# Key rows of both directions by seven block products, all but one ahead of the first burst of key matmuls

## The chip, the cores and the metric

The kernel runs on one core of a Trainium2 chip. The metric is the device time of one execution in microseconds. Three runs of the kernel before took 551.29, 551.41 and 551.92 us, a median of 551.41. Engines are named as in the profile: PE is TensorE's matmuls and PEld its weight loads, DVE is VectorE, ACT is ScalarE, POOL is GpSimd, and SP is the engine that issues most DMAs.

## The reference, cut to what matters

The inputs are `x` (16 batches of 512 nodes with 512 features), a condition vector for each batch, and a mask of 16 x 512 x 512 x 11 labels. For each of two directions, graph attention goes to the first 20 nodes only:

```
row_zero  = x.sum(-1) == 0
self_feat = concat(x, where(row_zero, 0, q)) @ W_self.T + b_self
output = self_feat
for d in range(2):
    A  = adj or adj transposed, first 20 columns      # 16 x 512 x 20 x 11
    vb = A @ w_bias + b_bias
    kv = self_feat[:, :20]
    qh = (self_feat @ Wq[d].T + bq[d])   in 16 heads of 32
    kh = (kv        @ Wk[d].T + bk[d])   in 16 heads of 32
    aff = where(A.sum(-1) > 0, qh . kh / sqrt(32), -9e15) + vb
    w   = softmax(aff over the 20)
    output += (w @ kv) @ Wout[d] per head + bout[d]
result = x + relu(output)
```

All of it is in float32. The change is about `kh`, the key rows, which are computed once for all batches.

## The kernel before, in words

**The whole.** A setup builds everything that the batches share, and then a loop runs over 16 batches. The order of the instructions on every engine is written out by hand (`manual_schedule`): an engine takes its instructions in the order in which the program emits them, and waits only for its operands and for the buffer that it writes.

**The setup.** Features lie on the 128 partitions in four chunks. The self features of the 16 x 20 = 320 key nodes come first: `kv_terms` (L767) multiplies `xkv` by the self weights `ws_v`; POOL and DVE multiply a flag by the projected condition (`qp`, L801); DVE adds the two (`kvn`, L805) and subtracts from each batch's nodes its first node (`kvD`, L809), which leaves 16 x 19 = 304 columns in four chunks. `kvT` (ACT, L813) is a copy with the bias for the value path.

**The key rows.** `key_rows(d, jc)` (L818) makes 128 rows of the keys of direction `d`: 4 chunks of 128 input features, each by four matmuls of 32 output columns, on 304 columns (L825); DVE then takes them out of PSUM into `khD` (L831). There are eight such blocks, two directions of four. Four of them are made ahead of the first burst, with the first three chunks of all four first; the other four go between the bursts 1 to 4.

**The bursts.** The keys must be multiplied by the query weights `wq_sb`, head by head. That is cut into 20 bursts (`keys`, L908). A burst fills four PSUM banks in two pairs (tags `s0` and `s1`, one buffer each), and then ACT takes one pair out (L939) and DVE the other (L941) into a staging tile `st`, which SP stores in DRAM (L946, L948) and whose part for batch 0 POOL copies (L945). The pairs have one buffer each, so the next burst starts when both are out. Between two bursts TensorE does something else from a plan written as letters: `m` bias terms (`bias_terms`, L838, DVE alone: query weights times the self bias, summed; they need `wq_sb` and `br_sb`), `b` their end (`biases`, L844, L846), `c` bias scores (L856), `v` and `w` pieces of the value products (`values`, L883), `n` row flags (L222), and `p` the seven block products of batch 0's self features (L284). When a value block is complete DVE takes it out (`value_pieces`, L896) and POOL's queue stores it (L900).

**Seven block products** are what the kernel uses already for the self features and for the scores: the matrix is cut in 2 x 2 blocks of 256 features by half the columns, and seven products of block sums replace eight. For that, `weight_sums` (L227 to L234) makes four sums of the self weight blocks on POOL, `ws_s`, between the `qp` multiplies and the row sums of batch 0 (`row_sums`, L215, L217). The `khD` rows of the changed kernel are made in the same way.

**What sets the order around the change.** On POOL: `rsk` (L761, L763), `qp` (L801), the four weight sums, `row_sums(0)`, then copies and stores between the bursts. On DVE: `qp`, `kvn` and `kvD` in turn, `qwD` (L814), the four `khD` rows, then the evictions of the bursts with bias terms and `khD` rows between them. On SP: the loads in the order in which they stand at L737 to L758, then `bo_rows` (L997) and the stores of the bursts.

Of the kernel before, what the change touches and what calls it, by code (L numbers as in the profile page):

```python
# [18 lines left out]
def gat_kernel(  # L19
# [99 lines left out]
    def load_adj(b, h, ins=None, ts=slice(0, 2)):  # L119
        if ts.start == 0:  # L120
            adjs[b, h] = load.tile([P, 2, S * L], I32, tag="adj", name=f"adj{b}_{h}", bufs=3)
        a = adj[b, h * 2 * P : (h + 1) * 2 * P].rearrange("(t p) d m l -> p t (d m l)", p=P)
        behind(nc.sync.dma_start(adjs[b, h][:, ts], a[:, ts]), ins)
# [100 lines left out]
        nc.vector.tensor_scalar(nzs[b], ps[:, :N], 0.0, None, ALU.not_equal)  # L224


    def weight_sums():  # L227

        (a11, a12), (a21, a22) = [[ws_v[:, 2 * j : 2 * j + 2, bass.ts(i, F // 2)] for j in range(2)] for i in range(2)]
        s1, s2, s3, s4 = (ws_s[:, i] for i in range(4))  # L230
        nc.gpsimd.tensor_add(s1, a21, a22)
        nc.gpsimd.tensor_sub(s2, s1, a11)
        nc.gpsimd.tensor_sub(s3, a11, a21)
        nc.gpsimd.tensor_sub(s4, a12, s2)  # L234

    def half(l):
        return slice(NG + l * HN, NG + (l + 1) * HN)
# [451 lines left out]
    with tc.tile_pool(name="setup", bufs=1) as sp, tc.tile_pool(name="ps_acc", bufs=4, space=PSUM) as acc["pool"]:  # L689
# [16 lines left out]
        kvD = sfp.tile([P, C, N], F32, tag="sf", name="kvD")[:, :, : B * ND]  # L706

        with tc.tile_pool(name="setup_k", bufs=1) as sk:
            xkv = sk.tile([P, C, BM], F32, name="xkv")
# [49 lines left out]


            nc.gpsimd.tensor_add(rsk, xkv[:, 0], xkv[:, 1])  # L761
            for k in range(2, C):
                nc.gpsimd.tensor_add(rsk, rsk, xkv[:, k])  # L763
            kv_ps = [bank(f"ps_kv{fc}") for fc in range(C)]

            def kv_terms(fc, k):
# [28 lines left out]
            )  # L795
            for fc in range(C):
                kv_terms(fc, 3)
            for fc in range(C):
                qp = sk.tile([P, B, NG], F32, tag="qp", name=f"qp{fc}", bufs=4)
                engine = nc.gpsimd if fc else nc.vector  # L800
                engine.tensor_mul(  # L801
                    qp, nzk.rearrange("p (b m) -> p b m", m=NG),
                    qw[:, fc].unsqueeze(2).to_broadcast([P, B, NG]),
                )
# [4 lines left out]
                nc.vector.tensor_sub(  # L809
                    kvD[:, fc].rearrange("p (b m) -> p b m", m=ND), each[:, :, 1:],  # L810
                    each[:, :, :1].to_broadcast([P, B, ND]),
                )
                nc.scalar.activation(kvT[:, fc], kvn[:, fc], AF.Identity, bias=bs_sb[:, fc : fc + 1])  # L813
            nc.vector.tensor_sub(qwD, qw[:, :2], qw[:, 2:])  # L814
            weight_sums()
            row_sums(0)

            def key_rows(d, jc, ks=range(C)):  # L818

                if ks[0] == 0:  # L820
                    of[d, jc] = bank(f"ps_k{d}{jc}")
                ps = of[d, jc]
                for k in ks:
                    for a in range(HL):
                        nc.tensor.matmul(  # L825
                            ps[bass.ts(a, R), : B * ND], wk_sb[d][:, k, bass.ds(jc * P + a * R, R)], kvD[:, k],
                            start=(k == 0), stop=(k == C - 1),
                        )
                if ks[-1] == C - 1:
                    by = bk_sb[:, d, jc : jc + 1]  # L830
                    nc.vector.tensor_scalar(khD[:, d * C + jc], ps[:, : B * ND], by, by, ALU.add, ALU.subtract)  # L831

            of = {}

            def bias_terms(d, c):

# [5 lines left out]
            def biases():  # L842

                nc.vector.tensor_add(bqw, bqw, bq_sb)  # L844
                for hl in range(HL):
                    nc.scalar.activation(  # L846
                        bqbd[bass.ts(hl, DH), :, :, hl], bqw[bass.ts(hl, DH)], AF.Copy, scale=SCALE
                    )

        with tc.tile_pool(name="setup_g", bufs=3) as sg:  # L850

# [98 lines left out]
            def block_product(n):  # L950
# [8 lines left out]


            steps = {
                "b": [(biases, ())],
                "c": [(bias_scores, (d,)) for d in range(2)],
                "m": [(bias_terms, (d, c)) for c in range(C) for d in range(2)],
                "n": [(row_flags, (b,)) for b in range(2)],
                "p": [(block_product, (n,)) for n in (1, 2, 6, 7, 5, 4, 3)],
                "v": [(values, (t, (d,), k)) for t in range(2) for d in range(2) for k in range(C)],
                "w": [(values, (2, (0, 1), k)) for k in range(C)],
            }
# [13 lines left out]
            rest = [(d, hg) for hg in range(C) for d in range(2)]  # L983
            first = None
            for r, k in ((0, 0), (1, 0), (0, 1), (1, 1), (2, 0), (2, 1), (0, 2), (1, 2), (3, 0), (3, 1), (2, 2), (3, 2)):
                key_rows(*rest[r], (k,))
            for r in range(4):
                key_rows(*rest.pop(0), (C - 1,))
            for n, runs in enumerate(bursts):
                for i in range(len(rest)):  # L990
                    if (i < 1 and n > 0) or any(fc == 0 and (d, hg) == rest[0] for fc, hg, d, _, _ in runs):
                        key_rows(*rest.pop(0))
                if n in (3, 4):
                    values(*steps["v"].pop(0)[1])
                if n == 0:
                    bo_rows = load.tile([P, C, N], F32, tag="x2", name="bo_rows", bufs=1)
                    nc.sync.dma_start(bo_rows[:, :2], bout.partition_broadcast(P))  # L997
# [6 lines left out]
                if rest:  # L1004
                    for kind in "mm" if n else ():
                        f, args = steps[kind].pop(0)
                        f(*args)
                    continue
                first = n if first is None else first
                for kind in plan[n - first] if n - first < len(plan) else ():  # L1010
                    f, args = steps[kind].pop(0)
                    f(*args)
                if n == first:
                    for d in range(2):
                        nc.gpsimd.tensor_add(br_sb, br_sb, bo_rows[:, d])
                if n > first:
                    value_pieces()
                if n == 7:
                    mask_mul(0, 0)
                if n == 8:  # L1020
# [376 lines left out]
```

## Time and profile before

| | |
|---|---|
| median of three runs | 551.41 us (551.29 to 551.92) |
| the profiled execution | 552.17 us |
| its span, first to last instruction | 550.3 us |
| mean granted TensorE clock | 0.996 |
| PE busy | 540.9 us (98%) |
| DVE busy | 480.0 us (87%) |
| POOL busy | 436.4 us (79%) |
| ACT busy | 404.4 us (73%) |
| first key row matmul | at 17.41 us |
| first burst | at 25.81 us |
| last product of the setup ends | at 92.11 us |

The span is counted from the first to the last instruction on the core; the execution's own time has some 1.9 us around it. Times of rows are microseconds from the span's start. A float32 matmul has two records in the trace, so 128 records are 64 matmuls. Weight loads (PEld) go on beside matmuls. The chain of waits is followed back from the last instruction, each step to what released it.

### The profile page before, as it was taken

How to read it: one execution, taken by the hardware profiler on the slowest of the kernel's cores; microseconds unless marked ns; L12 is line 12 of the kernel's file. 1: busy time of each engine (PE TensorE's matmuls, PEld its weight loads, DVE VectorE, ACT ScalarE, POOL GpSimd, SP SyncE). 2: the span in 40 equal slices, each digit the busy share in tenths (PEclk: the TensorE clock that was granted, in tenths of full speed). 3: DMA queues.
4: the chain of work that ended last, by engine and by line, in shares of the span. 5: the costliest groups of instructions: out<-in, count | busy, mean ns of one | idle time of the engine just before them, and what ended most of it. 6: DMA issues, size and time to landing. Idle time of an engine off the chain costs nothing.

```text
span 550.3 us, 19621 instructions
## 1 busy us (share of the span) xinstructions
PE 540.9 (98%) x7908; PEld 424.1 (77%) x7908; DVE 480.0 (87%) x708; ACT 404.4 (73%) x1000; POOL 436.4 (79%) x421
## 2 busy tenths in 40 slices
PE   9999999999999999999999999999999999999994
PEld 6554367888787878788888888887878788888783
DVE  0775678888989999999999999999999999999995
ACT  1125345798797988888888888887878787877663
POOL 2636896779979797979888888888897979797665
PEclk9999999999999999999999999999999999999998
DMA  8999999978887877878776767686777587736034
GB/s 301 375 396 350 306 357 348 298 224 242 227 253 210 219 229 224 231 209 234 208 237 181 241 188 222 203 228 192 231 207 212 175 252 189 229 103 187 2 117 154
DMA packets 100530, 126.45 MB, mean 230 GB/s; under 512 B 19592, under 2 KB 68678, under 8 KB 98392
## 3 DMA queue, kind: packets, MB, share of 16 engines
q1 hardware_dynamic: 98696, 121.93, 71.4%
q0 software_dynamic: 1168, 2.23, 1.7%
q8 instruction: 62, 1.02, 0.8%
q10 hardware_dynamic: 576, 1.05, 0.5%
q14 instruction: 28, 0.23, 0.1%
HBM read 86.23 MB, written 40.24 MB: 230 GB/s over the span
## 4 chain that ended last, share of the span: by engine, by line
PE 92%; DVE 4%; POOL 2%; issue 1%; ACT 0%; DVEq 0%; POOLq 0%; ACTq 0%
PE ps_f L657 30%; PE ps_a L397 23%; PE ps_c L397 11%; PE ps_d L397 6%; PE ps_o_f L567 5%; PE ps_v L883 3%; PE ps_k L825 3%; PE ps_o_c L567 2%; PE ps_kv L767 1%; PE ps_a L284 1%; PE ps_l L397 1%; POOL w L536 1%; PE ps_c L284 1%; PE ps_warm L727 1%; DVE cond L332 1%
## 5 line engine op out<-in xcount | busy, mean ns | idle before, releaser
L327 ACT ACTIVATE prod<-adj,wb_sb 128x80 f32<-128x80 int32 x330 | 116.0, 429 | 0.0
L536 POOL TENSOR_TENSOR w<-w,sm 128x640 f32<-128x640 f32 x63 | 80.3, 1274 | 30.6 <-DVE sm L532 29.4
L657 PE MATMUL ps_f<-t,ws_s 128*64 128x246 f32 x720 | 80.0, 371 | 0.0
L657 PEld LDWEIGHTS ps_f<-t,ws_s 128*64 128x64 f32 x720 | 51.8, 137 | 18.9
L527 ACT ACTIVATE w<-w 128x640 f32<-128x640 f32 x60 | 43.8, 730 | 18.5 <-DVE w L523 18.5
L544 DVE STREAM_TRANSPOSE wt<-w 128x640 f32<-128x640 f32 x63 | 52.5, 833 | 1.5 <-POOL w L536 1.4
L657 PE MATMUL ps_f<-x,ws_v 128*64 128x246 f32 x480 | 52.4, 371 | 0.0
L531 DVE TENSOR_REDUCE sm<-w 128x32 f32<-128x640 f32 x63 | 51.0, 810 | 1.1 <-ACT w L527 1.0
L522 DVE TENSOR_REDUCE ps_d<-w 128x32 f32<-128x640 f32 x59 | 48.7, 826 | 1.8 <-ACT ps_d L431 0.2
L523 DVE TENSOR_TENSOR w<-w,ps_d 128x640 f32<-128x640 f32 x59 | 48.4, 821 | 2.0
L657 PEld LDWEIGHTS ps_f<-x,ws_v 128*64 128x64 f32 x480 | 34.7, 137 | 13.0
L370 POOL TENSOR_TENSOR k<-g,k 128x608 f32<-128x608 f32 x30 | 44.7, 1490 | 0.0
L397 PEld LDWEIGHTS ps_a<-g,sf 128*64 128x64 f32 x544 | 34.2, 137 | 5.9 <-issue 5.8
L397 PE MATMUL ps_a<-g,sf 128*64 128x152 f32 x544 | 38.6, 295 | 0.0
L567 PE MATMUL ps_o_f<-wt,vd 32*32 32x256 f32 (+3 forms) x708 | 37.8, 383 | 0.3 <-ACT ps_o_f L554 0.3
L338 DVE TENSOR_REDUCE add<-prod 128x80 f32<-128x960 f32 x32 | 36.7, 1148 | 1.5 <-POOL prod L333 1.5
L397 PE MATMUL ps_d<-g,sf 128*64 128x152 f32 x544 | 37.9, 293 | 0.0
L346 ACT COPY both<-add 64x80 f32<-64x80 f32 x128 | 32.6, 255 | 5.7 <-DVE add L338 4.6
L567 PE MATMUL ps_o_c<-wt,vd 32*32 32x256 f32 (+1 forms) x720 | 36.8, 386 | 0.0
L672 POOL TENSOR_TENSOR t<-x,t 128x492 f32<-128x492 f32 x30 | 34.8, 1161 | 1.2
L333 POOL TENSOR_SCALAR prod<-cond 128x80 f32<-128x80 f32 x32 | 18.0, 564 | 22.1 <-DVE cond L332 20.8
L397 PEld LDWEIGHTS ps_d<-g,sf 128*64 128x64 f32 x544 | 35.3, 137 | 0.2 <-ACT sf L675 0.2
(298 smaller groups left out, 1437.8 us busy)
## 6 DMA issues: line engine op xcount, KB each, us to landing
g<-g_d SPq DMA_DIRECT2D x60, 304.0 KB
g_d<-st SPq DMA_DIRECT2D x16, 1064.0 KB
out_T<-o SPq DMA_DIRECT2D x63, 256.0 KB
x<-in_xT SPq DMA_DIRECT2D x56, 256.0 KB
xn<-in_xn SPq DMA_DIRECT2D x48, 256.0 KB
adj<-in_adj SPq DMA_DIRECT2D x52, 220.0 KB
vd<-bd_d SPq DMA_DIRECT2D x64, 64.0 KB
nz<-nz_d SPq DMA_DIRECT2D x14, 256.0 KB
```

What stands on the lines that cost most here:

```text
L327: nc.scalar.activation(p[:, :, l], a[:, :, l], AF.Identity, scale=wb_sb[:, l : l + 1])
L338: done["masks"] = nc.vector.tensor_reduce(add, prods.pop((b, h)), AX.X, ALU.add)
L370: done["ksum"] = engine.tensor_sub(to, one, two)
L397: nc.tensor.matmul(slot(g)[bass.ts(p, P // 2), : HL * S].rearrange("p (h m) -> p h m", m=NG)[:, :, 1:], of(k)[:, bass.ds(first + g * P // ...
L522: nc.vector.tensor_reduce(mx, f, AX.X, ALU.max)
L523: done["weigh"] = (engine or nc.vector).tensor_sub(f, f, mx.unsqueeze(2).to_broadcast([P, per, NG]))
L527: done["exp"] = nc.scalar.activation(t, t, AF.Exp)
L531: nc.vector.tensor_reduce(sm, heads(weighs[b, c, l]), AX.X, ALU.add)
L536: done["normal"] = nc.gpsimd.tensor_mul(f, f, smalls.pop((b, c, l)).unsqueeze(2).to_broadcast([P, per, NG]))
L544: done["turn"] = nc.vector.transpose(wts[b][:, c, l], weighs.pop((b, c, l)).rearrange("p g w -> p (g w)"))
L567: nc.tensor.matmul(outsum[b][a][bass.ds(at // 2 * DH, n * DH), bass.ds(c * N // 2 + lo * P, (hi - lo) * P)].rearrange("p (n r) -> p n r", ...
L657: nc.tensor.matmul(parts[b][n in (2, 3, 5)][bass.ts(a, P // 2), bass.ts(i, HN)], lhs, x[:, k], start=False, stop=k == 1, skip_group_check= ...
```

## The change

The key rows are made by seven products for each direction, cut like the self features: two halves of the input features, two halves of the output features, two halves of the 304 columns (152 each). `key_product(d, n)` is 8 matmuls of 128 x 64 weights on 152 columns; `key_rows(d, n)` adds product `n` into `khD` in two pieces, on ACT for products 1, 6 and 7, on DVE for 2, 5, 3 and 4. The products 1, 6, 7 and 4 share one PSUM bank, 5 and 3 another, 2 has one of its own. Four differences of `kvD` blocks (`kv_sum`, DVE) and four sums of weight blocks for each direction (`weight_sum`, POOL) are new.

Thirteen of the fourteen products stand ahead of the first burst, with all eight bias terms between them on DVE; the fourteenth follows burst 0. The sums of the self weights move behind bursts 3 to 6, in the buffer that held direction 0's key sums. The loads are in another order, and batch 1's `x` is loaded after the key products, because direction 1's key sums use its buffer. The value pieces start with burst 0 in place of burst 3.

```
-    def weight_sums():
-        (a11, a12), (a21, a22) = ...
-        nc.gpsimd.tensor_add(s1, a21, a22)
-        nc.gpsimd.tensor_sub(s2, s1, a11)
-        nc.gpsimd.tensor_sub(s3, a11, a21)
-        nc.gpsimd.tensor_sub(s4, a12, s2)
+    def weight_sum(w, s, n):
+        (a11, a12), (a21, a22) = [[w[:, 2 * j : 2 * j + 2, bass.ts(i, F // 2)] for j in range(2)] for i in range(2)]
+        if n == 1:
+            nc.gpsimd.tensor_add(s[:, 0], a21, a22)
+        else:
+            nc.gpsimd.tensor_sub(s[:, n - 1], *{2: (s[:, 0], a11), 3: (a11, a21), 4: (a12, s[:, 1])}[n])
...
+        wk_s = [ws_s, load.tile([P, 4, 2, F // 2], F32, tag="x1", name="wk_s1", bufs=1)]
...
             nc.sync.dma_start(br_sb, b_row.partition_broadcast(P))
+            nc.sync.dma_start(bq_sb, bq)
             load_x(0)
-            nc.sync.dma_start(wb_sb, w_bias.partition_broadcast(P))
-            load_adj(0, 0)
-            nc.sync.dma_start(bq_sb, bq)
-            nc.sync.dma_start(bb_sb, b_bias.partition_broadcast(P))
             for d in range(2):
                 rows(wo_sb[:, d], woT[d])
-            load_x(1)
+            bo_rows = load.tile([P, C, N], F32, tag="x2", name="bo_rows", bufs=1)
+            nc.sync.dma_start(bo_rows[:, :2], bout.partition_broadcast(P))
+            nc.sync.dma_start(wb_sb, w_bias.partition_broadcast(P))
+            nc.sync.dma_start(bb_sb, b_bias.partition_broadcast(P))
+            load_adj(0, 0)
             load_adj(0, 1)
             nc.gpsimd.tensor_add(rsk, xkv[:, 0], xkv[:, 1])
             for k in range(2, C):
                 nc.gpsimd.tensor_add(rsk, rsk, xkv[:, k])
+            for n in (1, 2):
+                weight_sum(wk_sb[0], wk_s[0], n)
...
+            def kv_sum(n):
+                one, two = {
+                    1: lambda: (kv_block(0, 1), kv_block(0, 0)), 2: lambda: (kv_block(1, 1), kv_sums[1]),
+                    3: lambda: (kv_block(1, 1), kv_block(0, 1)), 4: lambda: (kv_block(1, 0), kv_sums[2]),
+                }[n]()
+                nc.vector.tensor_sub(kv_sums[n], one, two)
             for fc in range(C):
...
+                if fc == 2:
+                    kv_sum(1)
+            for n in (2, 3, 4):
+                kv_sum(n)
+            for d, n in ((1, 1), (1, 2), (0, 3), (1, 3), (0, 4), (1, 4)):
+                weight_sum(wk_sb[d], wk_s[d], n)
-            nc.vector.tensor_sub(qwD, qw[:, :2], qw[:, 2:])
-            weight_sums()
             row_sums(0)
...
+            def key_product(d, n, ks=range(2)):
+                w, x = {
+                    1: ((0, 0), kv_block(0, 0)), 2: ((0, 1), kv_block(1, 0)), 3: (3, kv_block(1, 1)),
+                    4: ((1, 1), kv_sums[4]), 5: (0, kv_sums[1]), 6: (1, kv_sums[2]), 7: (2, kv_sums[3]),
+                }[n]
+                to = key_ps[d, "d" if n == 2 else "c" if n in (3, 5) else "a"]
+                for k in ks:
+                    for i in range(2):
+                        for a in range(2):
...
+                            nc.tensor.matmul(to[bass.ts(a, P // 2), bass.ts(i, KN)], lhs, x[:, k], ...)
+            def key_rows(d, n):
+                for i in range(2):
...
+                    if n == 4:
+                        nc.vector.tensor_scalar(to, ps, by, by, ALU.add, ALU.subtract)
+                    elif n in (1, 6, 7):
+                        nc.scalar.activation(to, ps, AF.Identity, bias=by)
+                    else:
+                        nc.vector.scalar_tensor_tensor(to, to, by, ps, ALU.subtract, ALU.add)
...
+            for k in range(2):
+                for d in range(2):
+                    key_product(d, 1, (k,))
+                    if k:
+                        key_rows(d, 1)
+            for n in (2, 6, 7, 5, 3):
+                for d in range(2):
+                    key_part(d, n)
+                    for _ in range({6: 2, 7: 1, 5: 1}.get(n, 0)):
+                        bias_terms(*terms_left.pop(0))
+            nc.vector.tensor_sub(qwD, qw[:, :2], qw[:, 2:])
+            for d in range(2):
+                nc.gpsimd.tensor_add(br_sb, br_sb, bo_rows[:, d])
+            key_part(0, 4)
+            biases()
...
-            plan = "mmvv bvv vvc vvc vvn vvw vw vw wn p p p p p p p".split()
+            plan = "kv vv vv vc vc vv vv vv vv vw ww wn n p p p p p p p".split()
...
             for n, runs in enumerate(bursts):
...
                 if n == 0:
-                    bo_rows = ...; nc.sync.dma_start(bo_rows[:, :2], bout.partition_broadcast(P))
+                    load_x(1)
                 keys(runs)
...
+                if 2 < n < 7:
+                    weight_sum(ws_v, ws_s, n - 2)
```

More of the change, by code (lines that the diff above doesn't have):

```diff
@@ L797, in gat_kernel, with kv_block @@
                 kv_terms(fc, 3)
+            KN = B * ND // 2
+            def kv_block(j, l):
+                return kvD[:, 2 * j : 2 * j + 2, bass.ts(l, KN)]
+            kv_sums = {n: sk.tile([P, 2, KN], F32, name=f"kv_t{n}") for n in range(1, 4)}
+            kv_sums[4] = kv_all[:, :2, B * ND : B * ND + KN]
+            def kv_sum(n):
[4 more added lines that the diff above has]
+                nc.vector.tensor_sub(kv_sums[n], one, two)
             for fc in range(C):
@@ L833, in gat_kernel @@
-            of = {}
+                if fc == 2:
[4 more added lines that the diff above has]
+                weight_sum(wk_sb[d], wk_s[d], n)
+            row_sums(0)
+            key_ps = {(d, "a"): bank(f"ps_k{d}") for d in range(2)}
+            for i, key in enumerate("dc"):
+                t = ps_s.tile([P, 2, 512], F32, tag=f"s{i}", name=f"ps_k{key}", bufs=1)
+                key_ps.update({(d, key): t[:, d] for d in range(2)})
@@ L848, in biases @@
                     )
+            terms_left = [(d, c) for c in range(C) for d in range(2)]
+            for k in range(2):
[13 more added lines that the diff above has]
+            biases()
         with tc.tile_pool(name="setup_g", bufs=3) as sg:
@@ L961, in gat_kernel @@
             steps = {
[L962 removed]
+                "k": [(key_part, (1, 4))],
                 "c": [(bias_scores, (d,)) for d in range(2)],
[L964 removed]
                 "n": [(row_flags, (b,)) for b in range(2)],
@@ L1003, in gat_kernel @@
                 value_pieces()
[L1004 to L1010, printed above, removed]
+                for kind in plan[n]:
                     f, args = steps[kind].pop(0)
                     f(*args)
[L1013 to L1017, printed above, removed]
+                value_pieces()
+                if 2 < n < 7:
+                    weight_sum(ws_v, ws_s, n - 2)
                 if n == 7:
```

47 lines of the change are left out of this document (19 added, 28 removed).

## The prediction, made before the result was known

> **What bounds the kernel now.** I read the busy shares of the page first, then the busy time by stretch of the start, then the chain of waits through it, then the DVE and POOL timelines of the stretch that the change rebuilds.
>
> ```profile
> span 550.3 us, 19621 instructions
> PE 540.9 (98%) x7908; PEld 424.1 (77%) x7908; DVE 480.0 (87%) x708; ACT 404.4 (73%) x1000; POOL 436.4 (79%) x421
> ```
> ```profile
> 20.00:25.00 5.00, 5.00 (x84) 2.60 (x80) 3.05 (x5) 0.56 (x1) 3.61 (x3) 1.00 1.05 381
> 25.00:30.00 5.00, 5.00 (x88) 2.72 (x76) 3.32 (x6) 1.07 (x2) 3.24 (x3) 1.00 1.07 373
> 30.00:35.00 5.00, 5.00 (x84) 2.58 (x83) 4.66 (x11) 2.21 (x5) 2.05 (x4) 1.00 1.05 384
> 75.00:80.00 5.00, 5.00 (x64) 3.54 (x64) 3.69 (x6) 3.04 (x6) 4.99 (x8) 1.00 1.02 347
> ```
> After the length of a stretch come PE, PEld, DVE, ACT and POOL busy. PE fills the start while DVE has 2 us of every 5 free until 30 us. So TensorE time saved is span saved, as long as TensorE isn't made to wait.
>
> ```profile
> 17.41 8.39 PE ps_k L825 x128
> 25.81 0.46 PE s_g(0, 0, 0, 0, 16)0_325 L917 x2
> ...
> 37.61 2.18 PE ps_k L825 x32
> ...
> 41.67 1.85 PE ps_v L883 x16
> ...
> 49.68 0.51 PE ps_c L856 x8
> ...
> 69.85 0.86 PE ps_nz L222 x8
> ...
> 92.11 2.22 PE ps_a L397 x32
> 94.33 2.07 PE ps_d L397 x32
> ```
> Start, length, what. The key rows start at 17.41, the first burst at 25.81, the last setup product ends at 92.11. Half the key rows (8.39) lie ahead of the first burst, the other four blocks (2.18 each, 8.72) between bursts.
>
> **The change, part by part.**
>
> *TensorE work.* Old: 8.39 + 8.72 = 17.1 us. New: 14 parts (seven products, two directions) of 8 matmuls, 128x64 against 152 columns. The score product at L397 has this very form: 2.07 us for 32 records, two a matmul, so 1.035 for eight. 14 x 1.035 = 14.5: 2.6 us less. 13 parts (13.5 us) go ahead of the first burst, so without a wait it starts at 17.41 + 13.5 = 30.9.
>
> *What they wait for.* This decides. Four block differences of kvD are new on DVE, with both inputs in SBUF, and the eight bias terms (L838, also two SBUF inputs) now stand ahead of the first burst. POOL gets two sums of the first key weights ahead of its qp multiplies, and six more behind them. So two-input DVE work meets a full POOL queue. What happens then the trace shows:
>
> ```profile
> 15.27 0.49 DVE L801 TENSOR_TENSOR qp<-nzk,qw 128x320 f32<-128x320 f32 x1
> 16.39 0.97 DVE L809 TENSOR_TENSOR kvD<-kvn 128x304 f32<-128x304 f32 x1
> 17.80 0.48 DVE L809 TENSOR_TENSOR kvD<-kvn 128x304 f32<-128x304 f32 x1
> 18.71 1.04 DVE L809 TENSOR_TENSOR kvD<-kvn 128x304 f32<-128x304 f32 x1
> 20.19 1.04 DVE L809 TENSOR_TENSOR kvD<-kvn 128x304 f32<-128x304 f32 x1
> 21.16 1.26 DVE L814 TENSOR_TENSOR qwD<-qw 128x32 f32<-128x32 f32 x1
> ```
> ```profile
> 11.16 0.86 POOL L763 TENSOR_TENSOR rsk<-rsk,xkv 128x320 f32<-128x320 f32 x1 [3.48 <-DMA xkv<-in_xkvT]
> 15.31 2.64 POOL L801 TENSOR_TENSOR qp<-nzk,qw 128x320 f32<-128x320 f32 x3 [3.29 <-DVE qw L792]
> 17.91 1.51 POOL L231 TENSOR_TENSOR ws_s<-ws_v 128x512 f32<-128x512 f32 x1
> 19.50 1.40 POOL L232 TENSOR_TENSOR ws_s<-ws_s,ws_v 128x512 f32<-128x512 f32 x1
> 20.86 1.51 POOL L233 TENSOR_TENSOR ws_s<-ws_v 128x512 f32<-128x512 f32 x1
> 22.34 1.28 POOL L234 TENSOR_TENSOR ws_s<-ws_v,ws_s 128x512 f32<-128x512 f32 x1
> 26.60 1.28 POOL L215 TENSOR_TENSOR rx<-x 128x512 f32<-128x512 f32 x1 [2.99 <-DMA x<-in_xT]
> ```
> The same kvD subtract takes 0.48 or 1.04. Each long one ends 0.33 behind the end of a POOL sum: 18.71 + 1.04 = 19.75, L231 ends 19.42; 20.19 + 1.04 = 21.23, L232 ends 20.90. The tiny L814 takes 1.26 and ends 0.05 behind L233 (22.37). So a two-input DVE instruction sits out the POOL instruction under way, runs 0.33, and POOL's next runs 1.15 behind it (19.75 to 20.90, 21.23 to 22.37). The bias term does so too:
>
> ```profile
> 43.10 0.64 POOL L945 COPY g<-st 128x152 f32<-128x152 f32 x1 [4.02 <-DVE st L941]
> ```
> ```profile
> 34.66 0.68 DVE L838 SCALAR_TENSOR_TENSOR bqt<-wq_sb,br_sb 128x512 f32<-128x512 f32 x1
> 35.27 0.68 DVE L838 SCALAR_TENSOR_TENSOR bqt<-wq_sb,br_sb 128x512 f32<-128x512 f32 x1
> 43.50 0.79 DVE L838 SCALAR_TENSOR_TENSOR bqt<-wq_sb,br_sb 128x512 f32<-128x512 f32 x1
> ```
> POOL ends at 43.74, this term at 44.29, 0.55 later; alone they follow each other in 0.61.
>
> *When POOL can start.* From the key inputs' last quarter (11.16) to x0 (26.60) 5.77 MB land (0.26 self weights, 2.1 key and 2.1 query weights, 0.26 bias, 1.05 x0, by the tiles' sizes), 374 GB/s. The first key weights, 1.31 MB behind 11.16, land at 14.7. The qp multiplies, at 15.31 now, wait for the two sums. With 1.25 for the first sum, 1.2 (between the 1.15 and 1.28 above) for the others, 0.77 a multiply ((2.64 - 0.33)/3), and one DVE instruction let in after each:
>
> | POOL (ends) | DVE let in behind it (ends) |
> |---|---|
> | key sums 1, 2 of direction 0 (16.0, 17.5) | qp0 (16.3), kvD0 (17.8) |
> | qp1, qp2, qp3 (18.6, 19.4, 20.5) | kvD1 (19.7), kvD2 (20.8) |
> | six key sums (22.0, 23.5, 25.05, 26.6, 28.1, 29.65) | difference 1 (22.3), kvD3 (23.85), differences 2, 3, 4 (25.4, 26.9, 28.45) |
>
> kvD3 is done at 23.85 in place of 21.23, and TensorE waits for it. The bound is then DVE's own row of work behind difference 4, whose short pieces cost by these rows:
>
> ```profile
> L297 DVE SCALAR_TENSOR_TENSOR sf<-nz,qw,ps_a 128x246 f32<-128x246 f32 x8 | 3.4, 467 | 1.6 <-PE ps_a L284 1.0 <-PE ps_a L289 0.6
> ```
> One PSUM input, no waiting for POOL: 0.467 at 246 columns, less 94 columns at 0.33/304 us each, gives 0.37 at 152, a pair about 0.6 (an estimate: two overlap a little). Then: two pairs of product 2 (28.45 to 29.7); bias terms 1 to 3, each let in behind one of the three row sums of x0 (L215: 30.85 POOL, 31.4; 33.1; 34.85); terms 4 to 6 alone (3 x 0.61: 36.7); product 5's pair, a term, its other pair, a term, product 3's two pairs (6 x 0.6: 40.3). Product 3 shares product 5's bank, so TensorE stops at 31.6 until 37.3; its two parts and the first direction's product 4 end at 40.65. That is the first burst's start: 9.75 behind 30.9.
>
> *The other edits.* ACT takes products 1, 6 and 7 out of PSUM in two pieces; TensorE has the other direction's 1.035 meanwhile: nothing (without that cover, some 0.8 a part, two pieces at about the 0.4 of DVE's above). Moving the first self-weight sums to bursts 3 to 6 puts 5.1 us (4 x 1.28) on POOL beside them and takes the bout adds out; POOL is full at 75 to 80 (4.99 of 5), so if that cover is short its x sums are late: 0 to 2.5, taken 0, because TensorE waits for POOL nowhere in these rows. The loads are put in another order on SP; x1 now waits there for the last key sum's reader, with only the g stores of later bursts behind it: nothing. Bursts: the evictions of one must end before the next, and these rows price it:
>
> ```profile
> 37.71 1.28 DVE L941 TENSOR_SCALAR st<-_g(0, 2, 0, 14, 16)1_450 128x76 f32<-128x76 f32 x3 [1.24 <-PE _g(0, 2, 0, 14, 16)1_450 L917]
> ```
> That burst ended at 37.61, so 1.4 us of other TensorE work are wanted between two. Two value pieces give 1.85 (L883), one and a bias score 0.93 + 0.51 = 1.44; burst 12 has only the row flags, 0.86 (the L222 row): 0.5 lost.
>
> *Sum.* First burst 40.65 - 25.81 = 14.84 later; 8.72 fewer between the bursts; the last part there 1.04; burst 12 0.5: **+7.65 us**. Profiled execution 552.17 (span 550.3, 1.9 around it), 0.76 over the median of 551.41. 552.17 + 7.65 - 0.76 = **559.1** as a median.
>
> *What the Trainium skill says.* SBUF — State Buffer, "Who interferes with whom": a VectorE instruction with two SBUF inputs contends with a GpSimd one that reads SBUF, and issue order decides who is shut out entirely. By that rule a waiting DVE instruction goes next, as in my table: +7.65. The trace mostly agrees, but once it doesn't:
>
> ```profile
> 92.79 1.49 POOL L370 TENSOR_TENSOR k<-g,k 128x608 f32<-128x608 f32 x1
> 94.23 1.07 POOL L672 TENSOR_TENSOR t<-x 128x492 f32<-128x492 f32 x1
> ```
> ```profile
> 92.86 3.00 DVE L377 TENSOR_TENSOR f<-sf 128x512 f32<-128x512 f32 x1
> ```
> DVE waited through two POOL instructions (95.30 + 0.56 = 95.86). Two such losses would add 2.3 to the sum, which I keep for the range.
>
> **The rivals.**
>
> *A half-lifted cover.* DVE gets in twice per POOL instruction as often as once. For: 0.48 at 17.80, which waited only 0.15. Against: L814. Without any waiting kvD3 comes at 21.23 as now, and TensorE has half a part and ten more behind it, 10.5 x 1.035: first burst at 32.1. Half way to my 40.65 is 36.4: 10.59 - 8.72 + 1.04 + 0.5 = **+3.4, 554.8**.
>
> *No waiting at all.* First burst at 32.1: 6.29 - 8.72 + 1.04 + 0.5 = **-0.9, 550.5**, no change that can be told. For it: DVE is idle 2 us of 5 now, so its work alone has room. Against it stand the long subtracts above.
>
> *TensorE never waits* and burst 12 costs nothing: 30.9, so 5.09 - 8.72 + 1.04 = **-2.6, 548.8**, faster. It decides only if POOL and DVE both finish ahead of TensorE; POOL's eleven instructions from 14.7 on speak against it.
>
> *The clock falls in the gap.* TensorE idles from 31.6 to 37.3 in my working. At the end of the kernel:
>
> ```profile
> 545.00:546.00 1.00, 0.00 (x0) 0.00 (x0) 1.00 (x4) 0.08 (x1) 0.72 (x1) 1.00 0.71 270
> 546.00:547.00 1.00, 0.00 (x0) 0.00 (x0) 0.54 (x2) 0.00 (x0) 0.00 (x0) 0.53 0.59 221
> ```
> the granted clock is 0.53 in the second microsecond without a matmul. Three parts at half speed cost 3 x 1.035 = 3.1 more: **+10.75, 562.2**. Against: the idle is broken up if DVE is quicker. The Trainium skill, TensorE: Matmul & The Clock Gate, Part 1, names an idle window of about 3.4 us for the drop to half rate; a gap of 5.7 would be over it, which is this rival.
>
> **How the numbers follow.** Forecast 0.55; clock 0.17; half-lifted 0.13; no waiting 0.08; never waits 0.07. A measurement can tell about 0.2%, 1.1 us, from no change. Slower 0.55 + 0.17 + 0.13 = 0.85, the same 0.08, faster 0.07. The range reaches from below the half-lifted case to just over the clock's, 553.3 to 562.6, which leaves out the 0.15 of the two quick cases and a little; the forecast's own is 557 to 561.4 (the two lost turns at its top).
>
> **What would show it.** Kv differences and late kvD subtracts on DVE of 1 us and more, each ending 0.33 behind a POOL sum; TensorE idle before product 2's second half and before product 3, put down to DVE; the first burst near 40; between bursts fewer gaps but one of half a microsecond at the second row flags. It is wrong if the differences take 0.48 each, or if the first burst comes before 34.

## The result, and the profile after

The changed kernel took 565.50 us (median of 4 runs, 564.35 to 565.93), the kernel before beside it 551.66 us (4 runs, 551.29 to 552.12): a ratio of 1.0247, with a 95% interval of 1.0235 to 1.026. The change makes the kernel 13.8 us slower. The sign was forecast; the size was not: 559.1 was predicted, and the range ended at 562.6.

The profiled execution took 565.08 us; the page gives its span and busy time.

```profile
span 563.2 us, 19606 instructions
PE 542.1 (96%) x7876; PEld 431.6 (77%) x7876; DVE 486.6 (86%) x720; ACT 408.4 (73%) x1012; POOL 446.9 (79%) x429
```

The span is 12.9 us longer (563.2 against 550.3), and PE's share fell from 98% to 96%. The busy time by stretch shows where; after the stretch's length come PE, PEld, DVE, ACT and POOL busy, the granted clock, the DMA share and GB/s.

```profile
20.00:25.00 5.00, 1.58 (x22) 1.02 (x18) 4.93 (x5) 1.68 (x6) 4.92 (x4) 1.00 1.06 380
25.00:30.00 5.00, 2.13 (x18) 2.00 (x20) 2.82 (x4) 0.00 (x0) 4.92 (x5) 0.59 1.05 388
30.00:35.00 5.00, 5.00 (x59) 4.74 (x57) 4.71 (x13) 1.67 (x6) 2.59 (x2) 0.72 0.87 307
75.00:80.00 5.00, 3.53 (x48) 1.85 (x44) 3.75 (x6) 1.42 (x5) 3.82 (x5) 1.00 1.01 366
...
25.00:26.00 1.00, 0.00 (x0) 0.00 (x0) 1.00 (x2) 0.00 (x0) 1.00 (x2) 0.97 1.04 389
26.00:27.00 1.00, 0.00 (x0) 0.00 (x0) 1.00 (x1) 0.00 (x0) 1.00 (x2) 0.50 1.06 395
...
32.00:33.00 1.00, 1.00 (x12) 0.95 (x10) 1.00 (x1) 0.67 (x2) 0.67 (x1) 0.61 1.04 357
```

PE was full in all four stretches before (5.00 of 5). Now it works 3.7 of the 10 us from 20 to 30, while DVE and POOL are full until past 27; and its clock is halved from 25.94 (0.97 of that microsecond is 0.94 at full speed and the rest at half) to 32.78 (0.61, counted the same way). From 75 to 80 it lacks 1.5 us again. PE's waits, in total, their number and the longest:

```profile
PE ps_kd L863 <- DVE khD L880: 4.2, 1, 4.2
PE ps_kc L863 <- DVE khD L880: 2.6, 3, 0.9
PE ps_kd L863 <- DVE kvD L829: 2.1, 1, 2.1
...
PE _g(2, 0, 1, 10, 16)1_782 L985 <- DVE st L1009: 1.5, 1, 1.5
...
PE _g(2, 2, 0, 14, 16)0_854 L985 <- ACT st L1007: 0.2, 1, 0.2
```

L863 are the key products; `ps_kd` holds product 2 of both directions, `ps_kc` products 5 and 3 of both. PE's timeline (start, length, what, and in brackets the idle time before and who ended it):

```profile
22.94 0.74 PE L863 MATMUL ps_kd<-kvD,wk 128*64 128x152 f32 x8 [2.10 <-DVE kvD L829]
27.87 2.29 PE L863 MATMUL ps_kd<-kvD,wk 128*64 128x152 f32 x16 [4.20 <-DVE khD L880]
29.95 2.24 PE L863 MATMUL ps_k<-kv_t,ws_s 128*64 128x152 f32 x16
...
35.49 1.23 PE L863 MATMUL ps_kc<-kv_t,ws_s 128*64 128x152 f32 x16
37.55 1.25 PE L863 MATMUL ps_kc<-kv_t,wk_s 128*64 128x152 f32 x16 [0.83 <-DVE khD L880]
...
44.03 0.53 PE L985 MATMUL s_g(0, 0, 0, 0, 16)0_422<-khD,wq_sb 32*128 32x304 f32 x2
...
45.08 1.25 PE L863 MATMUL ps_k<-kvD,wk 128*64 128x152 f32 x16
46.27 1.07 PE L951 MATMUL ps_v<-wo_sb,kvT 128*32 128x512 f32 x8
...
104.95 2.29 PE L396 MATMUL ps_a<-g,sf 128*64 128x152 f32 x32
```

And DVE and POOL, which TensorE waits for:

```profile
21.86 1.02 DVE L829 TENSOR_TENSOR kvD<-kvn 128x304 f32<-128x304 f32 x1
22.92 1.43 DVE L816 TENSOR_TENSOR kv_t<-kvD,kv_t 128x304 f32<-128x304 f32 x1
24.27 1.53 DVE L816 TENSOR_TENSOR kv_t<-kvD 128x304 f32<-128x304 f32 x1
25.72 1.53 DVE L816 TENSOR_TENSOR kvD<-kvD,kv_t 128x304 f32<-128x304 f32 x1
27.17 0.64 DVE L880 SCALAR_TENSOR_TENSOR khD<-khD,bk_sb,ps_kd 128x152 f32<-128x152 f32 x2
30.29 0.66 DVE L880 SCALAR_TENSOR_TENSOR khD<-khD,bk_sb,ps_kd 128x152 f32<-128x152 f32 x2 [2.47 <-PE ps_kd L863]
...
31.47 1.75 DVE L889 SCALAR_TENSOR_TENSOR bqt<-wq_sb,br_sb 128x512 f32<-128x512 f32 x1
...
75.94 0.69 DVE L964 SCALAR_TENSOR_TENSOR v<-br_sb,ps_v 128x512 f32<-128x512 f32 x1 [3.33 <-DMA vw_d<-v]
```
```profile
21.18 1.38 POOL L233 TENSOR_TENSOR wk_s<-wk_s,wk 128x512 f32<-128x512 f32 x1
22.51 1.50 POOL L233 TENSOR_TENSOR ws_s<-wk 128x512 f32<-128x512 f32 x1
23.97 1.49 POOL L233 TENSOR_TENSOR wk_s<-wk 128x512 f32<-128x512 f32 x1
...
26.88 1.50 POOL L233 TENSOR_TENSOR wk_s<-wk,wk_s 128x512 f32<-128x512 f32 x1
...
66.26 1.50 POOL L968 DMA_DIRECT2D vw_d<-v  x2
```

Direction 0's product 2 is done at 23.68. Direction 1's does not begin before 27.87, right behind the row pieces at 27.17 with which DVE took direction 0's out. Those stood on DVE behind the four block differences. After that the roles change: DVE's next piece (30.29, 2.47 us idle before it) waits for direction 1's product. Direction 1's product 2 needs neither `khD` rows nor any result of DVE that was late. What it shares with them is the tile.

So the first burst starts at 44.03 where it was 25.74 before and 40.65 was predicted. From there to the first score product of the loop (L396) 60.92 us pass; they were 66.31 before (L397, 92.05), and the prediction had 59.1. These are starts in the timeline, which all runs are compared by. The rows that the prediction shows (25.81 and 92.11) are of a view that puts the same starts 0.06 or 0.07 later; in that view the changed kernel has 44.10 and 105.02.

### The profile page after: what moved, and what is told of

It reads as the page before. It is cut to its first block, busy times and chain, and to the rows that moved or that the text cites. A ratio compares the mean times of both kernels' runs of the same rounds, so it can differ in the third digit from the quotient of the medians.

```text
span 563.2 us, 19606 instructions
## 1 busy us (share of the span) xinstructions
PE 542.1 (96%) x7876; PEld 431.6 (77%) x7876; DVE 486.6 (86%) x720; ACT 408.4 (73%) x1012; POOL 446.9 (79%) x429
## 3 DMA queue, kind: packets, MB, share of 16 engines
q8 instruction: 62, 1.02, 0.8%
## 4 chain that ended last, share of the span: by engine, by line
PE 84%; DVE 5%; POOL 4%; DMA 4%; issue 2%; ACT 1%; SPq 0%; DVEq 0%; POOLq 0%; ACTq 0%
PE ps_f L656 29%; PE ps_a L396 22%; PE ps_c L396 10%; PE ps_d L396 6%; PE ps_o_f L566 5%; DMA wk<-in_wkT 2%; PE ps_k L863 2%; DMA vw_d<-v 2%; PE ps_o_c L566 1%; PE ps_v L951 1%; PE ps_a L283 1%; PE ps_kc L863 1%; PE ps_l L396 1%; POOL cq_d L935 1%; POOL w L535 1%
## 5 line engine op out<-in xcount | busy, mean ns | idle before, releaser
L396 PEld LDWEIGHTS ps_a<-g,sf 128*64 128x64 f32 x544 | 34.2, 137 | 5.9 <-issue 5.8
L396 PE MATMUL ps_a<-g,sf 128*64 128x152 f32 x544 | 38.6, 295 | 0.0
L396 PE MATMUL ps_d<-g,sf 128*64 128x152 f32 x544 | 37.9, 293 | 0.0
L396 PEld LDWEIGHTS ps_d<-g,sf 128*64 128x64 f32 x544 | 35.3, 137 | 0.2 <-ACT sf L674 0.2
```

What stands on the lines that cost most here:

```text
L396: nc.tensor.matmul(slot(g)[bass.ts(p, P // 2), : HL * S].rearrange("p (h m) -> p h m", m=NG)[:, :, 1:], of(k)[:, bass.ds(first + g * P // ...
```

## The experiments

Each kernel was run beside the kernel before on the same chip. The table gives the start of the first burst, the time from there to the loop's first score product, the span (all three of the profiled execution), and the median and ratio of the timed runs.

| kernel | first burst | from there on | span | median | ratio to before |
|---|---|---|---|---|---|
| before | 25.74 | 66.31 | 550.3 | 551.66 | 1 |
| after | 44.03 | 60.92 | 563.2 | 565.50 | 1.0247 [1.0235, 1.026] |
| tiles by direction | 40.95 | 61.32 | 560.6 | 562.21 | 1.0184 [1.0163, 1.0206] |
| and bias terms between | 34.28 | 65.80 | 558.4 | 560.27 | 1.0161 [1.0144, 1.0178] |
| `x1` early | 43.76 | 60.58 | 562.6 | 565.66 | 1.0255 [1.0225, 1.0284] |
| unread matmuls | 42.95 | 61.00 | 562.7 | 565.14 | 1.0251 [1.0231, 1.027] |
| six key sums left out | 32.32 | 64.57 | 555.2 | 557.03 (one run) | |
| all together | 34.57 | 65.36 | 558.2 | 559.83 | 1.0146 [1.0128, 1.0164] |
| self sums first | 48.39 | 60.30 | 567.0 | 568.05 | 1.0291 [1.0241, 1.034] |
| row sums later | 36.41 | 60.32 | 555.0 | 557.54 | 1.0103 [1.0087, 1.0119] |
| combined | 38.09 | 61.05 | 557.5 | 559.10 | 1.0135 [1.0118, 1.0152] |

**Tiles by direction.** Is it the shared tile that makes the two directions take turns?

```
-            for i, key in enumerate("dc"):
-                t = ps_s.tile([P, 2, 512], F32, tag=f"s{i}", name=f"ps_k{key}", bufs=1)
-                key_ps.update({(d, key): t[:, d] for d in range(2)})
+            for d in range(2):
+                t = ps_s.tile([P, 2, 512], F32, tag=f"s{d}", name=f"ps_kx{d}", bufs=1)
+                key_ps.update({(d, key): t[:, i] for i, key in enumerate("dc")})
```

> One edit to the changed kernel: the two PSUM tiles that hold products 2 and products 5 and 3 are paired by direction (direction 0's two banks in one tile, direction 1's in the other) in place of by product. Theory A (the two directions wait for each other because their accumulators share a tile, so that TensorE and DVE take turns): direction 1's product 2 follows direction 0's at once near 24, no granted clock of 0.50 near 26 to 32, and the first burst comes at 39 to 40.5 in place of 44.1; the span falls by 3.5 to 5, to 558 to 560. Theory B (DVE's own row of work, bias terms and all, sets the first burst, and TensorE's turns only follow it): the first burst stays at 43 to 44 and the span within 1 of 563.2.

The first burst came at 40.95, 3.08 earlier and a little short of what was expected, and the median was 3.3 us below that of the changed kernel. The wait of 4.2 us is gone: the product of direction 1 follows that of direction 0 in one row, though DVE takes direction 0's out as late as ever (27.23). PE's and DVE's timelines of this kernel:

```profile
22.96 3.31 PE L863 MATMUL ps_kx<-kvD,wk 128*64 128x152 f32 x24 [2.08 <-DVE kvD L829]
...
36.03 1.81 PE L863 MATMUL ps_kx<-kvD,ws_s 128*64 128x152 f32 x16 [3.42 <-DVE khD L880]
```
```profile
28.97 1.75 DVE L889 SCALAR_TENSOR_TENSOR bqt<-wq_sb,br_sb 128x512 f32<-128x512 f32 x1
```

The order of the instructions is the same in both kernels, and no array moved but these halves. Nor is it the clock: it was halved for 6.8 us in both (25.94 to 32.78 there, 22.92 to 26.34 and 36.58 to 39.98 here). So the shared tile is the cause, and it costs about 3 us. It is not 4.2 + 2.6, because TensorE then meets the next wait: 3.42 us before product 3, the stop that the prediction had named. It stands behind bias terms on DVE, of which now three in a row are held by POOL's row sums of `x0` (the 1.75 above, then 1.76 and 1.74, in place of 0.68).

**Bias terms between the bursts again**, with tiles by direction. The plan's first letters become:

```
-            plan = "kv vv vv vc vc ..."
+            plan = "kvmm vvmm vvm vvm vvm vvmb vc vc vv ..."
```

> The tiles paired by direction as in the run before, and the eight bias terms put back between the first bursts (their buffer and the bias rows of the values in the free half of the bout tile). Theory A, with the bias terms as the next bound on DVE: product 3 no longer stops for them, the first burst comes at 34 to 35 and the span is 553 to 555. If the bias terms ahead of the burst cost nothing: the first burst and the span stay as in the run that only pairs the tiles by direction.

The first burst was as expected (34.28), the span was not (558.4 in place of 553 to 555): of the 6.67 us won there 4.48 were lost again between the bursts, and the median fell by 1.9. The last bias term and TensorE's waits on this kernel show it, in DVE's timeline, POOL's timeline, PE's waits and PE's timeline:

```profile
51.82 3.02 DVE L889 SCALAR_TENSOR_TENSOR bo_rows<-wq_sb,br_sb 128x512 f32<-128x512 f32 x1
```
```profile
51.77 1.28 POOL L233 TENSOR_TENSOR ws_s<-ws_s,ws_v 128x512 f32<-128x512 f32 x1
53.00 1.28 POOL L233 TENSOR_TENSOR ws_s<-ws_v 128x512 f32<-128x512 f32 x1
```
```profile
PE ps_c L920 <- ACT bqbd L897: 1.6, 1, 1.6
PE ps_nz L222 <- POOL rx L217: 1.6, 1, 1.6
```
```profile
76.12 1.78 PE L222 MATMUL ps_nz<-rx,ones 128*32 128x512 f32 x8 [1.61 <-POOL rx L217]
```

The term waits through two sums of the self weights, which the change had put there, and runs 0.56 past the second (54.84 against 54.28). The bias scores are late behind it, and the row flags behind POOL. TensorE's idle time between the bursts went from 2.52 to 5.28 us. The other 1.72 of the 4.48 are the clock, which fell behind these stops: it was 0.50 from 76.34 to 79.76, and the row flags at 76.12 took 1.78 (1.04 in the changed kernel). The other seven terms took 0.68 to 0.73, so a bias term was held only where POOL's self-weight sums had taken its cover.

**`x1` early.** The trace shows hardly any DMA from 35 to 44, since `x1`'s load stands on SP behind the last key sum's reader. Direction 1's key sums got another buffer and the load stands at its old place.

```
+            load_x(1)          # behind load_adj(0, 1)
...
-                if n == 0:
-                    load_x(1)
```

> One edit to the changed kernel: direction 1's key sums lie in a staging buffer that is free then, so that batch 1's x is loaded behind the masks as before and SP doesn't wait at 26 to 43. First burst as it was, at 44.1. If the empty DMA stretch (35 to 44) is what makes the late store of a value piece land after 8.6 us and DVE wait 3.3 us at burst 10, that wait goes and the span falls by 1.2 to 1.7. If POOL is the reason, because bias scores and self-weight sums stand ahead of the store in its queue, the wait stays at over 2 us and the span within 0.4 of 563.2.

Nothing measurable: 565.66 against 565.50, with the spans 0.6 apart. The value store landed almost as late as before: DVE's wait for it was 3.00 in place of 3.33. So the place of `x1`'s load costs nothing, as the prediction had it. This kernel too has a stretch with hardly any DMA (38 to 47), so the run does not tell what such a stretch costs.

**Unread matmuls** keep the clock up: four of 512 columns between the two parts of product 2, whose result nobody reads.

```
+                    if (n, d) == (2, 0):
+                        for _ in range(4):
+                            nc.tensor.matmul(warm2, ones, ws_v[:, 0], start=True, stop=True)
```

> One edit to the changed kernel: four matmuls of 512 columns whose result nobody reads stand between direction 0's and direction 1's product 2, in TensorE's gap from 23.7 to 27.8. The granted clock should stay at 1.00 through 26 to 33. If the half clock costs time by itself, the first burst comes 1.2 to 2.3 earlier (42 to 43) and the span falls as much; if DVE's turns hide it, both stay within 0.5.

The clock stayed at 1.00 through the gap, and each product took 1.04. The first burst came 1.08 earlier, less than expected, and the time did not change by what these runs can tell. PE's timeline shows why:

```profile
36.47 1.25 PE L863 MATMUL ps_kc<-kv_t,wk_s 128*64 128x152 f32 x16 [1.96 <-DVE khD L880]
```

TensorE now comes to product 5 earlier and waits 1.96 there, where it was 0.83. So of the half clock, worth 2.45 us of TensorE's work (27.87 to 32.78 at half speed), about half lay behind DVE anyway.

**Six key sums left out.** The bias-between kernel without POOL's six later key sums; products 3, 5, 6 and 7 read the raw key weights, so its keys are other numbers. This prices POOL's hold on DVE.

```
-            for d, n in ((1, 1), (1, 2), (0, 3), (1, 3), (0, 4), (1, 4)):
-                weight_sum(wk_sb[d], wk_s[d], n)
```

> Left out: the six later sums of key weights on POOL; products 3, 5, 6 and 7 of both directions read raw key weights in their place, so the keys are other numbers. Otherwise the kernel with tiles paired by direction and bias terms between the bursts, whose first burst comes at 34.35. If the wait for POOL's instructions is what stretches DVE's block differences (1.5 us each there), they now take 0.48, the last kvD subtract ends near 21.4 in place of 23.1, and the first burst comes at 32.2 to 32.8. If something else stretches them, they stay over 1 us and the burst stays near 34.3.

The differences on DVE:

```profile
21.28 0.47 DVE L817 TENSOR_TENSOR kv_t<-kvD,kv_t 128x304 f32<-128x304 f32 x1
21.67 0.47 DVE L817 TENSOR_TENSOR kv_t<-kvD 128x304 f32<-128x304 f32 x1
```

1.43 and 1.57 in the kernel with the sums beside them, 0.47 here, as expected: the hold is POOL's. But the first burst came only 1.96 us earlier (34.28 to 32.32), and nearly all of that is the last `kvD` subtract, done at 21.25 in place of 23.08. The longer differences cost TensorE hardly anything once the directions no longer shared a tile. The Trainium skill, SBUF — State Buffer, "Who interferes with whom", says that a VectorE instruction with two SBUF inputs contends with a GpSimd one that reads SBUF; 0.47 against 1.57 agrees.

**All together**: bias terms in bursts 1 to 4, the first key sums behind `qp`, `x1` early, and the self sums at bursts 0, 4 and 5.

```
+                for i in {0: (1, 2), 4: (3,), 5: (4,)}.get(n, ()):
+                    weight_sum(ws_v, ws_s, i)
```

> Tiles paired by direction, bias terms between bursts 1 to 4, both first key sums behind the qp multiplies, batch 1's x loaded early, and the self-weight sums at bursts 0, 4 and 5. By the theory (waits between the directions, DVE's row of work and two-input instructions waiting for POOL are the whole of it) the first burst comes at 32 to 33 and the span is 550 to 553, about the kernel before (550.3). If POOL falls short again between the bursts, as in the run with bias terms between the bursts (value stores, row sums of batch 1), the burst comes at 32 to 33 but the span is 555 or more.

The first burst (34.57) was 1.6 later than the top of what was expected. PE's timeline shows the clock in it:

```profile
21.79 3.31 PE L865 MATMUL ps_kx<-kvD,wk 128*64 128x152 f32 x24 [2.12 <-DVE kvD L831]
```

The same products took 1.77 in the kernel with the bias terms between, behind an idle time of 2.09. There the granted clock stayed at 1.00; here it was 0.50 from 21.76 to 25.16, worth 1.7 us of TensorE's work. Without them the burst would have been near 32.9, an estimate. Between the bursts it was the second of the two outcomes: `bqw`'s add took 3.20 us at 52.11, again behind POOL's sums, and TensorE waited 2.2 for the row sums and 1.6 for `bqbd`. So moving the self sums to these bursts moved what they held and freed nothing.

**Self sums first**: the changed kernel with the self-weight sums behind bursts 0 and 1. This tests the wait of 1.5 at burst 10: DVE takes a value block out at 75.94, and waits for the buffer's last store, issued on POOL at 66.26 behind bias-score stores and a self-weight sum.

```
-                if 2 < n < 7:
-                    weight_sum(ws_v, ws_s, n - 2)
+                if n < 2:
+                    weight_sum(ws_v, ws_s, 2 * n + 1)
+                    weight_sum(ws_v, ws_s, 2 * n + 2)
```

> One edit to the changed kernel: the four self-weight sums stand at bursts 0 and 1, where POOL is idle, in place of bursts 3 to 6. If POOL's queue is what sends the second value piece's store late (issued 66.3, landed 75.8, DVE waiting 3.3 and TensorE 1.5 at burst 10), the store is issued 1 to 2.6 earlier, TensorE's wait goes and the span falls by 1.2 to 1.8. If the transfer itself is what is slow, DVE waits as before and the span stays within 0.4 of 563.2. First burst at 44.1 either way.

DVE's wait fell from 3.33 to 1.43 and TensorE's at burst 10 is gone, but others of 0.9 and 0.5 came, for stores of the bursts. From the first burst on it took 0.62 less. The total cannot be read: the first burst stood at 48.39, though the edit touches nothing ahead of it. Part of that is 1.24 us by which product 2 already came later (29.11). PE's timeline has the rest:

```profile
39.05 1.25 PE L863 MATMUL ps_kc<-kv_t,wk_s 128*64 128x152 f32 x16 [0.83 <-DVE khD L880]
41.23 2.19 PE L863 MATMUL ps_kc<-kvD,ws_s 128*64 128x152 f32 x16 [0.92 <-DVE khD L880]
44.26 2.30 PE L863 MATMUL ps_kc<-kvD,wk_s 128*64 128x152 f32 x16 [0.84 <-DVE khD L880]
```

The same waits, but the clock fell a second time, at 41.4, and three parts ran at half speed. So the reason given for burst 10 is supported, not settled, and its price lies between some 0.6 and 1.5.

**Row sums later**: tiles by direction, and POOL's row sums of batch 0 behind burst 0.

```
-            row_sums(0)
...
+                if n == 0:
+                    row_sums(0)
```

> Tiles paired by direction (first burst 41.0 there) and, the one further edit, POOL's three row sums of batch 0 stand behind burst 0. If those row sums hold up the three bias terms of 1.75 us, these take 0.61 to 0.68 like the others, product 3 is freed 3 us earlier, the clock doesn't fall a second time, and the first burst comes at 36.5 to 38. If the terms are slow for another reason, 40.5 to 41.

As expected: all eight bias terms took 0.68, the first burst came 4.54 earlier than with the tiles alone, the clock fell once in place of twice, and nothing was given back between the bursts (60.32). Of the wait before product 3 (3.42) this is left in PE's timeline:

```profile
33.02 1.25 PE L862 MATMUL ps_kx<-kvD,ws_s 128*64 128x152 f32 x16 [0.18 <-DVE khD L879]
```

This is the best version with all its work in it, 5.7 us slower than the kernel before beside it (551.80).

**Combined**: four edits on top of the last, against TensorE's remaining stop (2.08 us for `kvD`) and the clock. The fourth, the self-weight sums behind bursts 0 and 1, is that of the run above.

```
-            for n in (1, 2):
-                weight_sum(wk_sb[0], wk_s[0], n)
...
+            for d in range(2):
+                key_product(d, 2, (0,))
+            for _ in range(1):
+                nc.tensor.matmul(warm2, ones, ws_v[:, 0], start=True, stop=True)
...
+                if n == 6:
+                    row_sums(0)
```

> The kernel of the run with the row sums behind the first burst, with four more edits: the first two key sums of direction 0 behind the qp multiplies on POOL, the first halves of product 2 of both directions ahead of the second halves with one unread matmul of 512 columns between them, the self-weight sums behind bursts 0 and 1, and the row sums of batch 0 behind burst 6. My theory: kvD3 ends near 21.8, the clock stays at full speed, and DVE's own row of work (four differences, the rows' pieces, eight bias terms) sets the first burst at 35.0 to 35.6 in place of 36.48; from the first burst to the loop's first score product 59 to 60.3, since DVE no longer waits for a value store; span 552.5 to 554, median 554 to 555.5, so still slower than the kernel before by 0.4 to 0.8%. Rival: without TensorE's waits ahead of the bursts the change is worth what the fewer products promise, first burst 33 or earlier, median 551.5 or less.

A miss: slower than the last, first burst 38.09, and 61.05 from there on where at most 60.3 was expected. PE's and DVE's timelines:

```profile
22.32 1.25 PE L860 MATMUL ps_kx<-kvD,wk 128*64 128x152 f32 x16 [0.55 <-DVE kvD L827]
...
33.31 2.29 PE L860 MATMUL ps_kx<-kvD,ws_s 128*64 128x152 f32 x16 [2.96 <-DVE khD L877]
35.36 1.76 PE L860 MATMUL ps_kx<-kvD,wk_s 128*64 128x152 f32 x16
```
```profile
28.36 1.77 DVE L886 SCALAR_TENSOR_TENSOR bqt<-wq_sb,br_sb 128x512 f32<-128x512 f32 x1
```

TensorE's early stop shrank to 0.55, as meant, and it was through with product 5 2.5 us sooner (29.11 + 1.23 = 30.34, against 32.83). It then stood 2.96 us before product 3, because DVE's row of work had not become shorter: it was 1.1 longer, by a bias term that now met the last key sum. The stop was long enough to halve the clock for product 3. Time won on TensorE ahead of a wait for DVE turned into more of that wait. As TensorE still stood, the rival of the expectation, that fewer products pay once it does not, stays untested. No version tried beats the kernel before.

## Why the prediction was right and wrong

**The step that failed** is "Product 3 shares product 5's bank, so TensorE stops at 31.6 until 37.3". It followed the banks within a direction only. The halves of one tile belong to the two directions, and direction 1's product 2 waited for DVE's take-out of direction 0's; the same for 5 and 3. In the working, product 2's two pairs both follow difference 4 with TensorE already gone on to product 6. In the trace TensorE stood for 4.2 us before direction 1's product 2, until DVE had taken direction 0's out, and then met three stops of at most 0.9 in place of one of 5.7. Undone alone, this is 3.08 us of first burst; the miss there was 3.45 (44.10 in the prediction's view, against 40.65).

**The lock of POOL on DVE** was right. The late `kvD` and the differences end 0.32 to 0.34 behind a POOL sum: 21.86 + 1.02 = 22.88 against 21.18 + 1.38 = 22.56; 24.35 against 24.01; 25.80 against 25.46. `kvD` was done at 22.88 (23.85 predicted), difference 4 at 27.25 (28.45). So DVE was 1.2 us quicker here than its table, and this may have made up for part of the failed step.

**DVE's row of work** was right in kind and arranged otherwise. Three bias terms were to be held by the row sums of `x0`; in the changed kernel one was (31.47, 1.75), as TensorE's own stop had pushed DVE past most of them. With tiles by direction all three were, and the first burst came at 40.95, 0.3 from the 40.65 forecast. So without the shared tile the forecast of this point would have held, though by luck, through two errors that nearly cancel: product 3 began there at 36.03, 1.3 ahead of the forecast, and the last three parts took 4.92 us in place of 3.35, because the clock had fallen.

**The clock's rival** was half right: it fell, in a gap of 4.2 us and not in the one of the working, and the parts behind it cost 2.45 of the 3.1 it was given. Kept up by unread matmuls, it gave 1.08 us of first burst and no time that the runs can tell, since DVE set the pace.

**Between the bursts** the sum had 8.72 fewer, 1.04 for the last part and 0.5 at burst 12, 59.1 in all against 60.92. The last part took 1.19 (45.08 to 46.27), burst 12 lost 0.2, and some 1.5 were lost at burst 10, most likely by the edit "0 to 2.5, taken 0": the argument was that TensorE waits for POOL nowhere. It does not, but it waits for DVE and DVE for a store. That the store is late by its place on POOL is supported by the run with the self sums first, and not settled. Some 0.45 stay unassigned.

**The sum**: 3.45 (first burst) + 0.15 (last part) - 0.3 (burst 12) + 1.5 (burst 10) + 0.45 = 5.25 over the forecast of 7.65, which makes the 12.9 by which the scores start later (105.02 against 92.11) and the span is longer. The median missed by more, 6.4 us (565.50 against 559.1). The forecast took 0.76 off because the profiled execution of before lay that much over its median; this one lies 0.42 under its own.

**The rivals with little or no waiting** had DVE's free time for them. That time was real in the rows of before and gone once POOL was full beside it: with no later key sums at all the first burst is at 32.32, about the 32.1 of "no waiting". But there the directions had tiles of their own and the bias terms stood between the bursts, and the loss between them (64.57) kept that kernel slower than before too.

## What to carry to other kernels

Before moving products ahead of a stage, write down for every PSUM tile who fills and who empties each part of it: here two independent streams in the halves of one tile took turns, and the rows of either alone did not show it. A queue that becomes the bound takes up whatever is won ahead of it, so take work off that queue, not off the engine that waits for it: POOL's row sums behind the first burst gave 4.54 us of first burst, TensorE's shorter stop in the combined kernel nothing. And work that has a free cover should not be moved in the same edit that gives the cover to something else. Whether the eight bias terms (0.61 each) were better left between the bursts no run here shows: put back, they met POOL's self-weight sums there, and the best version has them ahead.

## What the runs showed of the hardware that was not expected

**The clock falls and rises in steps of 3.42 us.** By the granted clock of single microseconds, the stretches at half speed last 6.84 us after the change (25.94 to 32.78). With tiles by direction these rows bound the first stretch:

```profile
22.00:23.00 1.00, 0.04 (x2) 0.04 (x2) 0.96 (x2) 1.00 (x4) 1.00 (x2) 0.96 1.03 375
23.00:24.00 1.00, 1.00 (x8) 0.95 (x10) 1.00 (x1) 0.56 (x2) 1.00 (x2) 0.50 1.10 399
...
26.00:27.00 1.00, 1.00 (x18) 0.97 (x16) 1.00 (x1) 0.00 (x0) 1.00 (x2) 0.83 1.04 385
```

22.92 to 26.34 is 3.42; the combined kernel's stretch, worked out alike from 33.06 to 36.48, is 3.42 too, and 6.84 is twice that. The Trainium skill, TensorE: Matmul & The Clock Gate, Part 1, tells of a free-running window of 3413 ns, and these lengths agree. But it speaks of an idle window for the fall. Here the 3.42 us ahead of 22.92 held only 2.0 us of idle time (20.88 to 22.92), so TensorE was busy for about 40% of them, and the clock fell at once; the same gap of 2.1 us ahead of 22.94 in the changed kernel let it stay at 1.00 until 25.94. Counted in stretches of 3.42 us from these edges, the clock fell behind those in which TensorE was busy for 22% (22.53 to 25.94 in the changed kernel), for these 40%, and for 49% (37.97 to 41.38 in the kernel with the self sums first). It did not fall behind 51% and 52% (19.11 to 22.53 and 36.20 to 39.61 in the changed kernel). So in these runs it was where a gap lies against the windows that mattered, and that differs from kernel to kernel with nothing changed near it, as the kernel with the self sums first shows. A gap of 2 us is enough to be unlucky.

**A DVE instruction can be shut out by two POOL instructions in a row.** The prediction had found one such row, 3.00 us at 92.86 in the kernel before, and kept it for its range. 3.02 and 3.20 us are recorded above, where a wait for one POOL instruction makes the row 1.5 to 1.75. Both times two POOL sums followed each other with no free time between them (the second time DVE's instruction came 0.66 us ahead of them, while POOL still issued a store), but so did the key sums, behind each of which DVE got in. What decides was not found.
